# A last part in another order, its mask partly added before the exponential, and one Gelu layer moved by three steps

## The chip, the core and the metric

The kernel runs on one core of a Trainium2 chip. The metric is the time of one execution on the device in microseconds (us); it is the median of several runs. TensorE (PE) multiplies matrices into PSUM, which has eight banks of 512 f32 per partition; VectorE (DVE) and ScalarE (ACT) read PSUM and SBUF; GpSimd (POOL) works on SBUF alone; SyncE (SP) issues most transfers. Each engine executes its own instructions in the order in which they were issued and waits for the others by semaphores.

## What is computed

Everything is f32. There are four batches of 256 query tokens with 256 channels and 4096 context tokens with 192 channels. Each batch goes through three parts, each added to its input:

```python
x = x + cross(norm(x), ctx)   # 16 heads of 16, 4096 keys; scores clipped to +-10000, softmax
x = x + self(norm(x))         # q and k normed by head; causal mask; softmax
x = x + slots(norm(x))        # below
# slots: h = gelu([x, mean slot] @ w1 + b1); logits = h @ w2 (64 slots)
#   alpha = softmax over the 8 best logits, 0 elsewhere
#   slot input = alpha^T x / alpha's column sums; one GRU step on the 64 slots
#   the slots attend to each other, norm, a projection; out = alpha @ slot values @ wo
```

The cross attention also replaces all its weights by 1/4096 if any of them is not a number.

## The kernel before

There are two programs in one. `fast` computes everything with softmaxes that subtract no maximum: it takes the exponential of the scores as they are, multiplies by the values beside a column of ones, and so has numerator and denominator in one sum. `exact` (L215 to L850) computes everything again from the inputs, with the maximum subtracted and the scores clipped. Between them stand these lines:

```python
    redo = fast(tc, a, out, k, const, x0)      # L879
    with tc.If(redo > 0):
        exact(tc, a, out, k)
```

`redo` is a count. Whenever `fast` divides by a softmax's denominators, it also copies them from PSUM into its tile `dens` (128 x 256: batch, which attention, channel half, token half, head). `tile_divide` (L1930) does so for one token half: from the bank it reads 8 denominators per partition and channel half (columns 16, 48, 80 ... 240), writes the quotients to `s.att`, and returns a function that copies the same columns of the same bank to `dens` when it is called. In `ending`, the names `put`, `put0` and `put1` are such functions. `all_in_range` (L1675) compares each entry of `dens` with 1e-10 and 1e15 and makes a 1 for every partition that has an entry outside; `count_bad` (L1687) adds these up by a matmul into `nbad`, which all engines load at the end as `redo`.

`exact` has, for each batch, two passes over the 4096 context tokens in eight chunks of 512. A chunk has 4 key tiles, 2 channel halves and 2 head groups, so 16 blocks of 128 x 1024 scores. In the first pass ACT copies the block to SBUF and DVE makes three tensor_tensor of 128 x 1024 (running maximum, a comparison of the block with itself, the maximum of these). Then POOL takes the maximum over the partitions (two `partition_all_reduce` of 128 x 2048 per batch). In the second pass DVE clips the block (a tensor_scalar from PSUM) and subtracts the maximum (a tensor_tensor), ACT takes the exponential, and PE multiplies by the values. Both passes use two PSUM buffers in turn, for scores, keys and values alike. A sum over all context chunks follows, then self attention token tile by token tile, and the slots part for all batches.

`fast` is one long loop. Per batch it has 16 pairs of key tiles ("pairs", p), and from the second batch on one more step (p = 6) for the self attention of the batch before. In each pair PE makes the scores (L165), ACT the exponentials (L1778, L1780), PE the products with the values of the pair before (L179). Everything else of the batch before (norms, projections, Gelu layer, routing, slots) is spread over these pairs by `plan`, keyed by batch, pair and place in the pair. An even pair also makes the next chunk's keys (L80, L86; moved to SBUF by DVE L94 and ACT L95), an odd one its values (L107, L120). The Gelu layer (`x2_turned`, then `hidden`, L1414) stands at pairs 9 and 10. ACT holds one table of functions; a change between Exp, Gelu and Sqrt is an instruction of its own (ACT_TABLE_LOAD).

In the last batch (b = 3) the last pairs work on token halves: pairs 13 to 16 use `tile_block` (L1876 to L1890) and `tile_weigh` (L1900). Pair 15 ends the first half's cross attention (`tile_out`), pair 16 begins its self attention (`tile_in`). `ending` (L2174) does the rest without any more cross scores to fill PE: the second half's cross attention, the self attention of both halves (`first_*`, `second_*`), norm, Gelu layer, routing (`chosen`), slot inputs, GRU (`gates`), slot attention, and the outputs of all four batches that are still due (`given_out`, `send`). `fill` issues matmuls on zeros. `banks` is one PSUM tile of eight banks; `x_0 ... w_1` are its banks, and the order of PE, DVE and ACT is exactly the order of the code.

Of the kernel before, what the change touches and what calls it, by code (L numbers as in the profile page):

```python
# [19 lines left out]
H, D = 16, 16  # L20
# [880 lines left out]
def fast_(es, tc, nc, a, out, k, const, x0):  # L901
# [180 lines left out]
    tri = kept.tile([P, P], F32, name="tri")  # L1082
    lng = kept.tile([D, 4], F32, name="lng")
# [44 lines left out]
    def set_plain(bank):  # L1128

        for i in range(2):  # L1130
            for c in range(2):
                w = wqkv[:, c, i * C : (i + 1) * C].rearrange("p (h d) -> p h d", d=D)
                m = small.tile([P, H], F32, name="wmean", tag="wmean")
                nc.vector.tensor_reduce(m, w, AX.X, ALU.add)
                nc.vector.tensor_scalar(m, m, 1.0 / D, None, ALU.mult)
                nc.vector.tensor_tensor(
                    w, w, m.unsqueeze(2).to_broadcast([P, H, D]), ALU.subtract
                )

        nc.tensor.transpose(bank[:, 0:P], tri, ident)  # L1140
        nc.vector.tensor_scalar(tri, bank[:, 0:P], 0.0, None, ALU.is_ge)
        for v in vself:
            ones_beside(nc, v)
        nc.vector.memset(sumto, 1.0 / C)
# [339 lines left out]
    def alpha_turned(s, bank):  # L1484
# [7 lines left out]
        nc.scalar.copy(s.two.alphaT[r], bank[r, 0:NQ])  # L1492
# [167 lines left out]
    def given_out(s, bank):  # L1660

        for t in range(QT):
            to = bank[:, t * C : (t + 1) * C]
            nc.tensor.matmul(
                to, ident, s.x2[:, t, :], start=(t == 0), stop=False, skip_group_check=True
            )
        for t in range(QT):
# [50 lines left out]
    for b in range(B - 1):  # L1718
# [20 lines left out]
            ((9, 0), step(x2_turned, s)),  # L1739
            ((HIDDEN_AT, 0), step(hidden, s)),  # L1740
# [152 lines left out]
    def tile_weigh(blocks, c, bank):  # L1893

        for k_, (v_, n, pr) in enumerate(blocks):
# [75 lines left out]
    def tile_stats(src):  # L1971
# [3 lines left out]
        nc.vector.bn_aggr(mv, st)  # L1975
        return mv

    def tile_variance(s, t):
# [4 lines left out]
        mv, var = tile_stats(s.xo[:, t, :]), s.var_t[:, t, 2 * H :]  # L1983
        nc.vector.tensor_scalar(var, mv[:, 1:2], EPS, BIG, ALU.add, ALU.min)
        nc.vector.tensor_scalar(s.eps_t[:, t : t + 1], var, EPS, None, ALU.mult)
# [15 lines left out]
    def tile_v(s, t, bank):  # L2001
        product(
            bank[:, 0:C],
            lambda c: s.x1T[:, c, t * P : (t + 1) * P],
            lambda c: wqkv[:, c, 2 * C : 3 * C],
        )
# [8 lines left out]
    def tile_heads(s, t, sq):  # L2015

        nc.vector.tensor_reduce(
            s.var_t[:, t, 0 : 2 * H], sq.rearrange("p (h d) -> p h d", d=D), AX.X, ALU.add
        )

# [8 lines left out]
    def tile_qk_turned(s, t, q, k_, *engines):  # L2029

        for i, bank in enumerate((q, k_)):
            for c in range(2):
                nc.tensor.transpose(
                    bank[:, c * P : (c + 1) * P],
                    s.qk[:, t, i * C + c * P : i * C + (c + 1) * P],
                    ident,
                )
        at = slice(t * P, (t + 1) * P)
        for dst, bank, i, eng in (
            (s.sq[:, :, 0, at], q, 0, engines[0]),  # L2040
            (s.sq[:, :, 1, at], q, 1, engines[1]),
            (s.sk[:, :, at], k_, 4, engines[2]),
        ):
            src = bank[:, 0 : 2 * P].rearrange("p (c q) -> p c q", c=2)
            j = i + (1 if i == 4 else 2)
            g, b_ = gb[:, i : i + 1], gb[:, j : j + 1]
            if eng is nc.vector:
                nc.vector.tensor_scalar(dst, src, g, b_, ALU.mult, ALU.add)
            else:
                nc.scalar.activation(dst, src, AF.Identity, bias=b_, scale=g)  # L2050
# [9 lines left out]
    def first_scores(s, pairs):  # L2060

        prs = []
        for c in range(2):
            for h in range(2):
                for m in range(2):
                    r = pair_rows(h, m)
                    nc.tensor.matmul(
                        pairs[h][:, m, c * NQ : (c + 1) * NQ],
                        s.sk[r, c, 0:P],
                        s.sq[r, c, :, 0:P],  # L2070
                        start=True,
                        stop=True,
                    )
        for h in range(2):
            pt = pp.tile([P, 2, 2 * NQ], F32, name="prob", tag="prob")
            nc.scalar.activation(pt, pairs[h], AF.Exp)
            prs.append(pt)
        return prs

    def first_weigh(s, prs, bank):  # L2080
        for c in range(2):
            for h in range(8):
                g, m, e = h // 4, h // 2 % 2, h % 2
# [4 lines left out]
                    prs[g][:, m, c * NQ + e * P : c * NQ + (e + 1) * P],  # L2088
# [5 lines left out]
    def second_scores(s, c, h, pair, j):  # L2094

        for m in range(2):
            r = pair_rows(h, m)
            nc.tensor.matmul(
                pair[:, m, j * NQ : (j + 1) * NQ],
                s.sk[r, c, j * P : (j + 1) * P],  # L2100
                s.sq[r, c, :, P:],
                start=True,
                stop=True,
            )

# [8 lines left out]
    def second_weigh(s, prs, c, bank):  # L2114
        for j in range(2):
            for h in range(8):
                g, m, e = h // 4, h // 2 % 2, h % 2
# [4 lines left out]
                    prs[g][:, m, j * NQ + e * P : j * NQ + (e + 1) * P],  # L2122
# [10 lines left out]
    def tile_out(x_0, x_1, y_0, y_1):  # L2133
# [14 lines left out]
        tile_variance(s, 0)  # L2148
# [7 lines left out]
    def tile_in(x_0, x_1, y_0, y_1):  # L2156
# [3 lines left out]
        tokens_turned(x_0, s.xo, 0)  # L2160
        tokens(s.x1T, x_0, 0, nc.vector.tensor_copy)
        alpha_turned(d, y_1)
# [3 lines left out]
        sq = tile_qk(s, 0, x_1)  # L2166
        tile_v(s, 0, y_0)
        tile_heads(s, 0, sq)
        heads_ = s.var_t[:, 0, 0 : 2 * H]
        nc.vector.tensor_scalar(heads_, heads_, 1.0 / D, s.eps_t[:, 0:1], ALU.mult, ALU.add)  # L2170
        s.rs0 = rsqrt(s.var_t[:, 0, :])
        tile_factors(s, 0, x_1, s.rs0[:, 0 : 2 * H])

    def ending(blocks, *pairs):  # L2174
# [24 lines left out]
        tile_weigh(blocks, 1, x_0)  # L2199
        tile_add(s, 1, x_0, 1)  # L2200
        tile_qk_turned(s, 0, z_0, z_1, act, act, act)
        tile_v_moved(s, 0, y_0, s.rs0[:, 2 * H :])


        for c, bank in enumerate((w_0, w_1)):
            tile_turn(tile_of(s.sums[c], 1), bank)
# [3 lines left out]
        for put in puts:  # L2210
            put(vec.tensor_copy)
        prs = first_scores(s, (z, w))
        project(s, wo, x_0, 1)
        tile_residual(s, x_0, 1)
        preload(AF.Sqrt)


        tokens_turned(y_1, s.xo, 1)
        tokens(s.x1T, y_1, 1, vec.tensor_copy)
        tile_mask(prs[0].rearrange("p m (u q) -> p m u q", q=P))  # L2220
        tile_variance(s, 1)
        sq = tile_qk(s, 1, x_1)
        tile_mask(prs[1].rearrange("p m (u q) -> p m u q", q=P))
        tile_v(s, 1, x_0)
        var = s.var_t[:, 1, :]
        rs = small.tile([P, 2 * H + 1], F32, name="rs_t", tag="rs_t", bufs=1)
        act.activation(rs[:, 2 * H :], var[:, 2 * H :], AF.Sqrt)
        tile_heads(s, 1, sq)
        nc.vector.tensor_scalar(
            var[:, 0 : 2 * H], var[:, 0 : 2 * H], BIG, None, ALU.min  # L2230
        )
        act.activation(
            rs[:, 0 : 2 * H], var[:, 0 : 2 * H], AF.Sqrt, bias=s.eps_t[:, 1:2], scale=1.0 / D
        )
        nc.vector.reciprocal(rs, rs)
        tile_factors(s, 1, x_1, rs[:, 0 : 2 * H])
        first_weigh(s, prs, z_0)
        sums0 = as_sums(z_0, 4, act.copy)
        preload(AF.Exp)
        for c in range(2):  # L2240
            tile_turn(sums0[:, 2 * c : 2 * c + 2, :], z_1, c)
        fill(w_0, 0.86)
        tile_qk_turned(s, 1, y_0, y_1, vec, vec, act)
# [3 lines left out]
        put(vec.tensor_copy)  # L2247


        for j in range(2):  # L2250
            for h, pair in enumerate((x_, y)):
                second_scores(s, 0, h, pair, j)
        p0 = [second_exp(pair) for pair in (x_, y)]
        tokens_turned(w_0, s.att, 0)
        with_abo(0)
        tokens(s.attT, w_0, 0, vec.tensor_copy)
        residual(0, w_1)
        second_mask(p0[0])
        p1 = []
        for h, pair in enumerate((x_, y)):  # L2260
            for j in range(2):
                second_scores(s, 1, h, pair, j)
            p1.append(second_exp(pair))
        project(s, awo, w_1, 0, alone=False)
        second_mask(p0[1])
        mv0 = tile_stats(w_1[:, 0:C])
        rs2 = small.tile([P, 2], F32, name="rs2_t", tag="rs2_t", bufs=1)
        nc.vector.tensor_scalar(rs2[:, 0:1], mv0[:, 1:2], EPS, BIG, ALU.add, ALU.min)
        with_abo(1)
        second_weigh(s, p0, 0, z_0)  # L2270
        sums0 = as_sums(z_0, 2, vec.tensor_copy)
        second_mask(p1[0])
        preload(AF.Sqrt)
        residual(1, w_0)
        act.activation(rs2[:, 0:1], rs2[:, 0:1], AF.Sqrt)
        second_mask(p1[1])
        second_weigh(s, p1, 1, z_1)
# [262 lines left out]
```

## Time and profile before

| what | us |
|---|---|
| median of three runs (850.6 to 852.13) | 851.98 |
| the profiled execution | 850.88 |
| its span in the profile | 849.1 |
| PE busy in the span | 826.4 |
| ACT busy | 606.0 |
| DVE busy | 307.3 |

The profile shows `fast` alone: none of its groups comes from the lines of `exact`. It is read from the page's shares first, then from the chain of waits, which follows the work that ended last back from the end, and then from the timeline of the stretches that the change touches. From 0 to about 780 us the chain stays on PE; from there to the last output transfer, issued at 842.93 us, it goes from engine to engine.

### The profile page before, as it was taken

What the parts mean: (1) busy time and instruction counts of PE and PEld (TensorE: products, weight loads), DVE (VectorE), ACT (ScalarE), POOL (GpSimd) and SP (SyncE); (2) the same over time, 40 slices, a digit from 0 to 9 for tenths busy, and PEclk for the clock granted to TensorE, in tenths of its full rate; (3) what the DMA queues carried; (4) which work ended last, traced back from release to release, by engine and by line L of the source; (5) the groups of instructions that cost most, each with busy time, mean ns of one, the idle gap of its engine ahead of it and who ended that gap; (6) DMA issues with size and microseconds to landing.
All of it is one profiled execution on the core that took longest, in us unless ns stands there. A gap on an engine that the chain in (4) does not pass through costs nothing.

```text
span 849.1 us, 19377 instructions
## 1 busy us (share of the span) xinstructions
PE 826.4 (97%) x8403; PEld 451.4 (53%) x8403; DVE 307.3 (36%) x776; ACT 606.0 (71%) x841; POOL 16.8 (2%) x20
## 2 busy tenths in 40 slices
PE   8999999999999999999999999999999999999886
PEld 5445555545555545545545555554545554567564
DVE  3123234222263353212253353232344442113654
ACT  5776776767677768777778777766778777777542
POOL 1000100000000010000000010000000000000000
PEclk9999999999999999999999999999999999999999
DMA  7601001000000000000000000000000000000001
GB/s 205 138 27 50 26 22 55 27 26 25 26 26 26 2 26 26 26 25 27 27 25 26 2 26 26 26 25 10 19 25 26 27 25 25 2 3 2 2 1 54
DMA packets 21822, 25.86 MB, mean 30 GB/s; under 512 B 6241, under 2 KB 13281, under 8 KB 21729
## 3 DMA queue, kind: packets, MB, share of 16 engines
q1 hardware_dynamic: 20784, 23.75, 9.6%
q8 instruction: 68, 1.11, 0.5%
q10 hardware_dynamic: 848, 0.79, 0.3%
q14 instruction: 26, 0.21, 0.1%
q0 software_dynamic: 96, 0.01, 0.0%
HBM read 23.48 MB, written 1.05 MB: 29 GB/s over the span
## 4 chain that ended last, share of the span: by engine, by line
PE 93%; DVE 3%; ACT 2%; issue 1%; DVEq 0%; ACTq 0%
PE banks L165 28%; PE banks L179 25%; PE banks L993 7%; PE banks L80 7%; PE banks L107 7%; PE banks L86 4%; PE banks L120 4%; PE banks L1876 2%; PE banks L1900 1%; PE banks L981 1%; PE banks L1843 1%; PE banks L1058 1%; PE banks L1812 1%; PE banks L194 1%; ACT prob L1780 1%; PE banks L1461 1%
## 5 line engine op out<-in xcount | busy, mean ns | idle before, releaser
L1780 ACT ACTIVATE prob<-banks 128x1024 f32<-128x1024 f32 x360 | 343.8, 1043 | 0.0
L165 PE MATMUL banks<-qh,kt 32*128 32x512 f32 x1920 | 250.2, 620 | 1.2 <-DVE qh L1036 1.2
L179 PE MATMUL banks<-prob,v 128*32 128x256 f32 x3840 | 219.6, 381 | 0.8 <-ACT prob L1822 0.5
L1778 ACT ACTIVATE prob<-banks 128x512 f32<-128x512 f32 x240 | 130.3, 595 | 121.7 <-PE banks L165 121.4
L179 PEld LDWEIGHTS banks<-prob,v 128*32 128x32 f32 x3840 | 118.6, 110 | 117.0 <-ACT prob L1778 42.8
L165 PEld LDWEIGHTS banks<-qh,kt 32*128 32x128 f32 x1920 | 97.6, 183 | 111.1 <-issue 62.5
L1794 DVE TENSOR_TENSOR sums<-banks,sums 128x512 f32<-128x512 f32 x112 | 77.1, 691 | 178.4 <-PE banks L179 155.8
L107 PE MATMUL banks<-wv,ctx 128*128 128x256 f32 x256 | 61.6, 384 | 0.0
L80 PE MATMUL banks<-ctx,wk 128*128 128x512 f32 x128 | 61.5, 603 | 0.1
L107 PEld LDWEIGHTS banks<-wv,ctx 128*128 128x128 f32 x256 | 46.8, 190 | 14.2 <-ACT prob L1778 6.8
L150 DVE COPY v<-banks 128x512 f32<-128x512 f32 x35 | 23.9, 691 | 81.6 <-PE banks L120 77.2
L94 DVE TENSOR_SCALAR kt<-banks,bk 128x512 f32<-128x512 f32 x32 | 24.0, 751 | 66.9 <-PE banks L86 66.8
L150 ACT COPY v<-banks 128x512 f32<-128x512 f32 x29 | 17.0, 587 | 30.0 <-PE banks L120 28.8
L120 PE MATMUL banks<-wv,ctx 64*128 64x256 f32 x256 | 36.3, 402 | 0.0
L86 PE MATMUL banks<-ctx,wk 64*128 64x512 f32 x128 | 36.1, 641 | 0.0
L95 ACT ACTIVATE kt<-banks,bk 128x512 f32<-128x512 f32 x32 | 22.1, 690 | 17.9 <-PE banks L86 17.1
L80 PEld LDWEIGHTS banks<-ctx,wk 128*128 128x128 f32 x128 | 20.9, 189 | 21.2 <-ACT prob L1780 12.1
L120 PEld LDWEIGHTS banks<-wv,ctx 64*128 64x128 f32 x256 | 22.0, 186 | 11.1 <-issue 9.3
L1822 ACT ACTIVATE prob<-banks 128x512 f32<-128x512 f32 (+1 forms) x30 | 17.9, 693 | 8.5 <-PE banks L1812 8.5
L987 DVE COPY tmp<-banks 128x512 f32<-128x512 f32 x17 | 11.8, 691 | 32.8 <-PE banks L981 32.8
L1890 ACT ACTIVATE prob<-banks 128x1024 f32<-128x1024 f32 x24 | 22.9, 1043 | 0.0
L993 PE MATMUL banks<-wqkv,tmp 128*128 128x256 f32 (+1 forms) x56 | 19.6, 482 | 0.5 <-ACT prob L1822 0.5
(310 smaller groups left out, 601.4 us busy)
## 6 DMA issues: line engine op xcount, KB each, us to landing
ctx<-in_ctxT SPq DMA_DIRECT2D x32, 256.0 KB, 3.0
ctx<-in_ctxT SPq DMA_DIRECT2D x64, 128.0 KB, 3.2
x<-in_x SPq DMA_DIRECT2D x4, 256.0 KB, 3.3
wih<-in_ffn_WihT SPq DMA_DIRECT2D x1, 768.0 KB, 7.1
tmp<-in_ffn_WhhT SPq DMA_DIRECT2D x3, 256.0 KB, 4.1
out<-tmp SPq DMA_DIRECT2D x3, 256.0 KB, 2.4
wq<-in_L_xattn_Wq ACTq DMA_DIRECT2D x1, 256.0 KB, 5.6
wo<-in_L_xattn_Wo SPq DMA_DIRECT2D x1, 256.0 KB, 4.7
```

Source lines behind the costliest of these rows:

```text
L80: nc.tensor.matmul(pk[c], k.wk[:, 0, c * P : (c + 1) * P], cx[:, 0, :], start=True, stop=False)
L86: nc.tensor.matmul(pk[c], k.wk[left(c), 1, c * P : (c + 1) * P], cx[left(c), 1, :], start=False, stop=True,)
L94: nc.vector.tensor_scalar(kt[:, 0, :], pk[0], k.bk[:, 0:1], None, ALU.add)
L107: nc.tensor.matmul(pv[n // 2][:, n % 2, :], cx[:, 0, n * P : (n + 1) * P], k.wv[:, 0, :], start=(n % 2 == 0), stop=False, skip_group_check ...
L120: nc.tensor.matmul(pv[u][:, i, :], cx[left(u), 1, n * P : (n + 1) * P], k.wv[left(u), 1, :], start=False, stop=True, skip_group_check=True,)
L150: copy(v[:, :, 0 : H * VW].rearrange("p i (h w) -> p i h w", w=VW)[:, :, :, 0:D], src.rearrange("p i (h d) -> p i h d", d=D),)
L165: nc.tensor.matmul(sc[:, m, :], kt[r, c, i * P : (i + 1) * P], qh[r, c, :], start=True, stop=True)
L179: nc.tensor.matmul(po[q * 32 : (q + 1) * 32, s * NQ : (s + 1) * NQ], v[:, i, w0 : w0 + 32], pr[s][:, m, e * NQ : (e + 1) * NQ], start=(fir ...
L993: nc.tensor.matmul(dst, lhs(c), rhs(c), start=(c == 0), stop=(c == 1))
L1778: nc.scalar.activation(pt[:, m, :], sc[:, m, :], AF.Exp)
L1780: nc.scalar.activation(pt, sc, AF.Exp)
L1794: nc.vector.tensor_tensor(s.sums[c], bank, s.sums[c], ALU.add)
```

## The change

The change has four parts. (1) The third batch's `x2_turned` moves from pair 9 to pair 12 and its `hidden` from pair 10 to pair 13, behind the keys of the last chunk (a new place 3). (2) `tile_in` takes the roots by ACT's table instead of the DVE iteration and uses other banks. (3) `ending` is reordered: scores, exponentials and weighing by head group; for two of the four second-half blocks the causal mask is a summand that PE puts into the bank before the scores (`second_hidden`); the `fill` calls in it are gone; the tables are loaded ahead of their use. (4) The outputs of batches 0 and 1 move forward, and `residual_out` is split off `given_out`. The diff, cut to its core:

```diff
+        nc.vector.tensor_scalar(
+            hidden_by, tri, 2.0**100, -(2.0**100), ALU.mult, ALU.add
+        )
...
-            ((9, 0), step(x2_turned, s)),
-            ((HIDDEN_AT, 0), step(hidden, s)),
+            ((9 if b < B - 2 else 12, 0), step(x2_turned, s)),
+            ((HIDDEN_AT, 0) if b < B - 2 else (13, 3), step(hidden, s)),
...
+    def tile_roots(s, t, sq):
+
+        var = s.var_t[:, t, :]
+        rs = small.tile([P, 2 * H + 1], F32, name="rs_t", tag="rs_t", bufs=1)
+        nc.scalar.activation(rs[:, 2 * H :], var[:, 2 * H :], AF.Sqrt)
         nc.vector.tensor_reduce(
-            s.var_t[:, t, 0 : 2 * H], sq.rearrange("p (h d) -> p h d", d=D), AX.X, ALU.add
-        )
+            var[:, 0 : 2 * H], sq.rearrange("p (h d) -> p h d", d=D), AX.X, ALU.add
+        )
+        nc.vector.tensor_scalar(var[:, 0 : 2 * H], var[:, 0 : 2 * H], BIG, None, ALU.min)
+        nc.scalar.activation(
...
+    def second_hidden(pair):
 
         for m in range(2):
             nc.tensor.matmul(
+                pair[:, m, NQ : 2 * NQ],
+                ident,
+                hidden_by.unsqueeze(1).to_broadcast([P, 2, P]),
                 start=True,
+                stop=False,
+                skip_group_check=True,
+            )
...
         tokens_turned(x_0, s.xo, 0)
+        move = alpha_turned(d, x_1, True)
         tokens(s.x1T, x_0, 0, nc.vector.tensor_copy)
-        alpha_turned(d, y_1)
...
-        sq = tile_qk(s, 0, x_1)
+        sq = tile_qk(s, 0, x_0)
         tile_v(s, 0, y_0)
-        tile_heads(s, 0, sq)
-        heads_ = s.var_t[:, 0, 0 : 2 * H]
-        nc.vector.tensor_scalar(heads_, heads_, 1.0 / D, s.eps_t[:, 0:1], ALU.mult, ALU.add)
-        s.rs0 = rsqrt(s.var_t[:, 0, :])
-        tile_factors(s, 0, x_1, s.rs0[:, 0 : 2 * H])
+        move()
+        s.rs0 = tile_roots(s, 0, sq)
+        preload(AF.Exp)
+        nc.vector.reciprocal(s.rs0, s.rs0)
+        tile_factors(s, 0, x_0, s.rs0[:, 0 : 2 * H])
...
-        fill(w_0, 0.86)
-        tile_qk_turned(s, 1, y_0, y_1, vec, vec, act)
+        for i, bank in enumerate((w_0, w_1)):
+            tile_turned(s, 1, i, bank)
+        tile_moved(s, 1, 0, w_0, vec)
+        tile_moved(s, 1, 1, w_0, vec)
+        tile_moved(s, 1, 4, w_1, act)
...
+        second_hidden(y)
+        second_scores(s, 1, 1, y, True)
+        p11 = second_exp(y)
+        preload(AF.Sqrt)
+        second_mask(p01)
+        second_weigh(s, p00, 0, 0, w_0)
+        second_weigh(s, p01, 0, 1, w_0)
+        second_mask(p10)
+        sums0 = as_sums(w_0, 2, vec.tensor_copy)
+        project(s, awo, x_0, 0, (0,), alone=False)
+        second_weigh(s, p10, 1, 0, w_1)
+        second_weigh(s, p11, 1, 1, w_1)
+        tile_turn(sums0, z_0)
+        sums1 = as_sums(w_1, 2, vec.tensor_copy)
+        residual(1, w_0)
+        put0 = tile_divide(s, z_0, (0,), 1, 1)
+        tile_turn(sums1, z_1)
...
-        tile_turn(sums0, x_0)
-        put0 = tile_divide(s, x_0, (0,), 1, 1)
-        tile_turn(sums1, y_0)
-        tokens_turned(x_1, s.att, 1, (0,))
-        tokens(s.attT, x_1, 1, act.copy, (0,))
-        put1 = tile_divide(s, y_0, (1,), 1, 1)
+        tokens_turned(y_0, s.att, 1, (0,))
+        tokens(s.attT, y_0, 1, act.copy, (0,))
+        put1 = tile_divide(s, z_1, (1,), 1, 1)
         tokens_turned(y_1, s.att, 1, (1,))
...
-        gelu0 = hidden_product(0, x_1)
-        fill(y_1, 0.43)
-        tokens_turned(z_1, s.x2n, 1)
+        gelu0 = hidden_product(0, w_1)
+        tokens_turned(z_0, s.x2n, 1)
+        preload(AF.Gelu)
         gelu0()
-        tokens(s.x2nT, z_1, 1, vec.tensor_copy)
+        tokens(s.x2nT, z_0, 1, vec.tensor_copy)
+        logits(s, 0, x_1[:, 0:SLOTS])
+        gelu1 = hidden_product(1, z_1)
+        gelu1()
+        preload(AF.Exp)
+        act.copy(s.x2[:, 0, :], x_0[:, 0:C])
         act.copy(s.x2[:, 1, :], w_0[:, 0:C])
-        hidden_product(1, w_1)()
-        with_bias(s, "x2", s.x2, fbo)
         put0(vec.tensor_copy)
         put1(vec.tensor_copy)
...
-        slot_inputs(d, z_0, z_1)
-        fill(x_1, 0.86)
+        slot_inputs(d, w_1, z_0)
+        given_out(batches[0], y_0)
         finish(route)
-        slot_inputs(s, y_1, w_0)
-        alpha_turned(s, w_1)
-        finish(gates(both_, x_1, z_1, y_0))
+        with_bias(s, "x2", s.x2, fbo)
+        slot_inputs(s, z_1, x_1)
+        alpha_turned(s, w_0)
+        finish(gates(both_, w_1, z_0, y_1))
         check_range = all_in_range()
         next(check_range)
-        given_out(batches[0], x_0)
-        slot_qk(both_, y_1, w_0)()
+        residual_out(batches[1], x_0)
+        given_out(batches[1], x_0)
...
         finish(mixing)
+        preload(AF.Sqrt)
         move()
-        kept_slots(both_, z_1)
-        at_turned(both_, y_1)
-        given_out(batches[1], z_0)
-        count_bad(y_0)
+        kept_slots(both_, w_1)
+        at_turned(both_, z_1)
+        count_bad(y_1)
...
+            take(3, y[:, 1, :])
             take(4)
```

## The prediction

> **What bounds the kernel now.** The page first: PE is busy for 97% of the span, and all of it is `fast`; no line of `exact` is among the groups.
>
> ```profile
> span 849.1 us, 19377 instructions
> PE 826.4 (97%) x8403; PEld 451.4 (53%) x8403; DVE 307.3 (36%) x776; ACT 606.0 (71%) x841; POOL 16.8 (2%) x20
> ```
>
> Then the chain of waits, in order of time. Up to 780 us it lies on PE, but for places such as the Gelu layer of pair 10, where ACT loads two tables and PE's next products (L179) start at 721.33:
>
> ```profile
> 714.73 2.86 ACT prob L1780 x3
> ...
> 717.60 1.28 ACT L1414
> ...
> 718.90 0.47 ACT hT L1414
> ...
> 719.39 1.28 ACT L1778
> ...
> 720.68 0.60 ACT prob L1778
> ```
>
> Behind 780 it changes engine at almost every step, and PE's own order costs time too: the reader sees two matmul groups of an output (L1664, L1646) between the transpose L1583 and its consumer L1600.
>
> ```profile
> 835.48 0.33 PE banks L1583
> 835.81 0.87 PE banks L1664 x4
> 836.67 1.06 PE banks L1646 x4
> 837.73 0.12 PE banks L1688 x2
> 837.85 0.66 PE banks L1600 x4
> ```
>
> Last the timeline around the two deferred copies of denominators (L1942), because the change gives them other banks:
>
> ```profile
> 818.92 0.42 DVE L1952 COPY tmp<-banks 128x256 f32<-128x256 f32 x1 [0.94 <-PE banks L1946]
> 819.04 0.37 ACT L2328 COPY x<-banks 128x256 f32<-128x256 f32 x1
> 819.26 0.23 DVE L1942 COPY dens<-banks 128x8 f32<-128x8 f32 x2
> ```
>
> They run behind the copy of x2n's transposes. Before, they read x_0 and y_0, which hold the turned sums until the logits go there (L1417, 819.95).
>
> **The change, part by part: the order.** *Gelu layer.* Pair 10's step from L179 to L179 falls from 12.33 (709.00 to 721.33) to the plain odd pair's 10.56 (731.94 to 742.50): -1.77. At pair 13 PE waits in the trace for the keys' copies (751.18 to 752.13); hidden's matmuls (1.06) will fill that. But ACT will do, after its keys (751.89), a load, Gelu and a load (1.28 + 0.47 + 1.28 and gaps: 754.98) before the first exponential, whose half (0.60) is done at 755.6, and L1900 waits for it: from 754.07 to 755.6, +1.5. Exponentials have caught up by the next block, as ACT idles 1.8 there. The transposes (0.59) only change place. Net -0.2; with no catching up +1.
>
> *tile_in.* qk no longer waits behind alpha for the exponential of y (782.79): 783.41 becomes 782.5. Square, reduce, root by table (1.28 load + 0.5) and reciprocal end the factors at 788.5, not 790.04; weighing covers most of it, so 0.5 is kept at the copy of attT (792.40).
>
> *The reordered ending.* Projecting between two halves of the first scores gives 1.0; the sums copied by halves and no fill (0.86) in front of the q and k transposes 0.9; two masks fewer on DVE (0.69 each) against two matmul pairs of 1.06 for the summand, and weighing by head group, 0.7. The second token's x2n ends at about 814.9, not 817.99: -3.1. Logits follow on the same pattern, -3.0.
>
> *Outputs.* `given_out(batches[0])` stands in front of the exponentials of the routing: ACT takes its copy first, so PE's 1.34 + 1.06 and the copy's 0.59 lie before them. The gain shrinks to -1.6 at alpha. Behind the slot attention the two groups of 0.87 and 1.06 shown above go to an earlier wait: -1.6. Sum of the order: -0.2 - 1.6 - 1.6 = -3.4; bounds -6 and +3.
>
> The tables weigh against this: the row shows 1.28 and the next ACTIVATE 0.02 later. The Trainium skill ("ScalarE: Activation LUTs", "What ACT_TABLE_LOAD costs") has a drain of 1.38 beside each; with it the two added loads would cost 2.7 us more, and the order would gain about 1.
>
> **What the order does to the data.** `put0` now reads z_0, `put1` z_1, still at the end of the norm. By then `tokens_turned(z_0, s.x2n, 1)` has overwritten all 256 columns of z_0, and `hidden_product(1, z_1)` the first 128 of z_1. DVE executes the copy of x2n's transposes from z_0 just before put0, as in the timeline above, so put0 can't come earlier. It thus writes into `dens` 8 x 128 values of x2n. A normed token has mean zero over its channels, so about half of these are negative and fail >= 1e-10: `least` is 1 on nearly every partition, `nbad` about 128, `redo` > 0, and `exact` runs behind all of `fast`. No number above hides that; it is added whole.
>
> **What `exact` costs.** No row shows it; I count its instructions and price them by the nearest rows. There are 4 x 8 x 4 x 2 x 2 = 512 blocks in each pass.
>
> ```profile
> L2053 DVE TENSOR_TENSOR prob<-prob,tri 128x1024 f32<-128x1024 f32 x2 | 2.4, 1216 | 0.0
> ...
> L150 DVE COPY v<-banks 128x512 f32<-128x512 f32 x35 | 23.9, 691 | 81.6 <-PE banks L120 77.2 <-ACT prob L1890 4.5
> ```
>
> - DVE passes: 3 + 2 = 5 operations of 128 x 1024 per block, 2560. A tensor_tensor takes 1.216, and the next can begin 1.13 after it (796.63 to 797.76). The clip from PSUM: 0.691 for 512 columns and (1.216 - 0.688) for 512 more, 1.22, the same. ACT needs 1.04 per block, PE 0.25 per score matmul (L165) and 0.06 per record of L179, some 1 us per block: both hidden. 2560 x 1.13 = 2893 if all overlap, x 1.25 = 3200 if each waits for the one before. I take 1.16, near the overlapped row, since the two kinds alternate: 2970.
> - DVE per chunk: 64 halves of keys x 0.75 + 32 of values x 0.69 = 70.
> - Chunk borders of the second pass: keys and values take PE 3.0 each (748.15 to 751.18, 759.71 to 762.70) in the two buffers that the scores need; DVE has some 4 of other work meanwhile. 0 to 6 each; I take 2 x 32 = 64.
> - POOL's maximum over partitions: 8 of 128 x 2048, with DVE waiting. POOL's 128x512 takes 1.27, so one pass over 2048 is 5.1; seven halvings of 128 partitions would be 36. Geometric middle 14: 112 (41 to 288). Clip and memset of 128x4096 around it: 20.
> - The rest, with rows of the same shapes: inputs, norm and queries 27; context sums 32 x 2.4 (two buffers, 3.0 landing, 1.2 reduce) = 77; projection, norm, q and k 88; self attention 32 groups x 4.5 (DVE 1.9 to 3.3, ACT 2.3 to 3.0, half hidden) = 143; output projection 12; slots part 92. 439, bounds 300 and 600.
>
> Sum: 2970 + 70 + 64 + 112 + 20 + 439 = 3675. All low ends give 3324, all high 4370.
>
> **The total** is made against the profiled execution, 850.88 (0.13% under the median 851.98): 850.88 - 3.4 + 3675 = 4522; rounded up for the branch, 4530. The medians' 1.1 is nothing beside that.
>
> **Rivals.**
> 1. *`exact` doesn't run* (not slower). It needs `dens` to hold only values in range: if the copies saw the turned sums still in z_0 and z_1. For it speaks only that the bank's names are easily misread; against it the order of DVE's instructions. Then the order alone decides: 850.88 - 3.4 = 847.5, or 848.6 at the median, faster by 0.4%. It decides as soon as no value written is out of range.
> 2. *`exact` runs but isn't bound by DVE.* If PE fell to half clock in the passes, its 2.65 per pair of blocks (4 x 0.25 + 16 x 0.056 + 6.0 / 8) would be 5.3 against DVE's 4.6, +0.7 x 256 = 180 in the second pass; with POOL at its upper bound +176. 4530 + 356 = about 4890. For it: POOL's price is unknown, and PE is busy for a sixth of the first pass. Against: a busier PE should recover, and the granted clock stays at 1.00 in this trace until 845.1, 3.2 after the last matmul; PE's gaps in the first pass are 3.4 - 0.5 = 2.9. The Trainium skill ("TensorE: Matmul & The Clock Gate", "What's actually happening") halves the clock after an idle window of about 3.4; by that rule the clock would hold, just, and this rival would lose its first half.
> 3. *`exact` runs at the fast ends*: 1.13 per operation (-77), no border stalls (-64), POOL 41 (-71), the rest 380 (-59): 4530 - 271, about 4260.
> 4. *No `exact`, and the order loses*: pair 13 doesn't catch up and half-empty gaps of 2.4 without fill slow PE: up to 854.
>
> **How the numbers follow.** Chances: the forecast, 4330 to 4900, 0.80; above it (rival 2 and worse) 0.09; below, still with `exact` (rival 3), 0.06; rival 1 0.04; rival 4 0.01. The range 4330 to 4900 is the forecast's own: from three quarters of the way to rival 3 up to rival 2. Slower by over 0.2% (1.7 us, about what a measurement can tell from no change): 0.80 + 0.09 + 0.06 + 0.005 = 0.955; faster 0.04; within 0.2% 0.005. The predicted time is 4530.
>
> **What would show it.** In the profile after: lines L377 to L406 head the groups, tensor_tensor of 128x1024 by the 1500, DVE busy over 80%, PE below 60% of the span; POOL with eight long operations, which give its price. The step between two first-pass blocks is 3.4 to 3.5 and between two pairs of the second 4.6. The `fast` part ends its last DVE addition near 839, not 842.9; the Gelu layer's load stands behind the keys of pair 13. Wrong it would be by a span near 846 with no line of `exact`, or by a POOL operation far outside 5 to 36.

## The result, and the profile after

The changed kernel takes 4624.2 us (median of four runs, 4615.21 to 4626.31) against 851.64 before (850.6 to 852.13): 5.4286 times as long, 95% interval 5.4192 to 5.438. The profiled execution took 4615.21, with a span of 4613.4. The page (shares and the row of the granted clock in 40 slices):

```profile
span 4613.4 us, 47479 instructions
...
PE 3433.4 (74%) x18909; PEld 1337.1 (29%) x18909; DVE 3584.8 (78%) x3998; ACT 1836.9 (40%) x2309; POOL 161.2 (3%) x94
...
PEclk9999999655558775555787555577865556886697
```

There are 2.5 times as many instructions as before, and from the eighth slice (of 115 us) on the clock is another: this is where `fast` ends. The costliest groups of DVE and POOL (columns: line, tiles, count, then busy time, mean ns, and idle time before):

```profile
L378 DVE TENSOR_TENSOR top<-top,raw 128x1024 f32<-128x1024 f32 x512 | 623.6, 1218 | 71.3 <-ACT raw L377 71.3
...
L402 DVE TENSOR_SCALAR gprob<-ring 128x1024 f32<-128x1024 f32 x512 | 603.9, 1215 | 13.7 <-PE ring L165 13.4
...
L383 POOL PARTITION_ALL_REDUCE shift<-top x8 | 83.9, 10539 | 2907.6 <-DVE top L378 2907.6
```

L215 to L850 are `exact`, of which the page before had no line. The timeline of the changed kernel's DVE shows what calls it:

```profile
816.65 0.42 DVE L1965 COPY tmp<-banks 128x256 f32<-128x256 f32 x1 [0.53 <-PE banks L1959]
817.00 0.16 DVE L1955 COPY dens<-banks 128x8 f32<-128x8 f32 x1
818.80 0.17 DVE L1955 COPY dens<-banks 128x8 f32<-128x8 f32 x1 [1.65 <-ACT hT L2372]
```

The first line reads x2n's transposes from z_0; the next, `put0`, takes its 8 "denominators" from the same bank. The third, `put1`, even waits 1.65 for the hidden product that ACT reads in z_1. Time by stage (columns: stretch, its length, busy time and instructions of PE, weight loads, DVE, ACT, POOL, then granted clock, DMA share, GB/s). The four rows are the first and the second pass of the first batch, the context sums, and all the rest of `exact`:

```profile
879.20:1356.00 476.80, 289.88 (x594) 79.61 (x592) 448.25 (x395) 135.12 (x137) 21.04 (x2) 0.53 0.03 9
1356.00:1715.20 359.20, 298.77 (x1720) 92.03 (x1720) 307.00 (x284) 145.90 (x145) 0.00 (x0) 0.79 0.04 12
...
4206.00:4290.00 84.00, 11.28 (x28) 4.71 (x20) 43.42 (x57) 0.00 (x0) 0.00 (x0) 0.50 0.55 175
4290.00:4613.40 323.40, 240.19 (x1214) 188.37 (x1214) 197.19 (x431) 105.72 (x335) 55.41 (x64) 0.78 0.08 23
```

`fast` ends its last addition at 844.60 (843.91 and 0.69); 34.6 go into `exact`'s loads, norm and queries; the eight passes take 3326.8 (four of about 477, four of about 356); then 84.0 and 323.4. So nearly all of the difference is `exact` (3768.8 to the span's end). But the last addition of `fast` is also later than the 842.90 of before, where the prediction had it near 839. The experiments go after both.

### The profile page after: what moved, and what is told of

The parts are those of the page before. It is cut to its first block, busy times and chain, and to the rows that moved or that the text cites. A ratio compares the mean times of both kernels' runs of the same rounds, so it can differ in the third digit from the quotient of the medians.

```text
span 4613.4 us, 47479 instructions
## 1 busy us (share of the span) xinstructions
PE 3433.4 (74%) x18909; PEld 1337.1 (29%) x18909; DVE 3584.8 (78%) x3998; ACT 1836.9 (40%) x2309; POOL 161.2 (3%) x94
## 4 chain that ended last, share of the span: by engine, by line
DVE 50%; PE 36%; ACT 6%; issue 3%; POOL 3%; DMA 1%; SPq 0%; ACTq 0%; DVEq 0%; POOLq 0%
DVE top L378 12%; DVE ne L379 12%; DVE nan L380 12%; PE ring L165 7%; DVE gprob L402 6%; PE banks L165 5%; ACT gprob L406 5%; PE banks L179 5%; DVE gprob L403 4%; PE po L179 3%; POOL shift L383 2%; PE ring L80 2%; PE ring L86 1%; PE banks L993 1%; PE banks L80 1%
## 5 line engine op out<-in xcount | busy, mean ns | idle before, releaser
L165 PE MATMUL ring<-qh,kt 32*128 32x512 f32 x4096 | 1533.0, 998 | 729.6 <-ACT raw L377 506.5
L377 ACT COPY raw<-ring 128x1024 f32<-128x1024 f32 x512 | 515.1, 1012 | 1093.9 <-DVE ne L379 1046.6
L165 PEld LDWEIGHTS ring<-qh,kt 32*128 32x128 f32 x4096 | 424.6, 269 | 1644.4 <-ACT raw L377 1168.3
L406 ACT ACTIVATE gprob<-gprob 128x1024 f32<-128x1024 f32 x512 | 541.0, 1057 | 678.6 <-DVE gprob L403 508.1
L378 DVE TENSOR_TENSOR top<-top,raw 128x1024 f32<-128x1024 f32 x512 | 623.6, 1218 | 71.3 <-ACT raw L377 71.3
L379 DVE TENSOR_TENSOR ne<-raw 128x1024 f32<-128x1024 f32 x512 | 623.5, 1218 | 0.0
L380 DVE TENSOR_TENSOR nan<-nan,ne 128x1024 f32<-128x1024 f32 x512 | 623.3, 1217 | 0.0
L402 DVE TENSOR_SCALAR gprob<-ring 128x1024 f32<-128x1024 f32 x512 | 603.9, 1215 | 13.7 <-PE ring L165 13.4
L403 DVE TENSOR_TENSOR gprob<-gprob,shift 128x1024 f32<-128x1024 f32 x512 | 604.7, 1217 | 2.0
L179 PE MATMUL po<-gprob,g_v 128*32 128x256 f32 x4096 | 403.3, 473 | 220.2 <-ACT gprob L406 215.2
L179 PEld LDWEIGHTS po<-gprob,g_v 128*32 128x32 f32 x4096 | 88.8, 120 | 689.7 <-ACT gprob L406 646.8
L179 PE MATMUL banks<-prob,v 128*32 128x256 f32 x3840 | 219.6, 381 | 0.5 <-ACT prob L1834 0.5
L179 PEld LDWEIGHTS banks<-prob,v 128*32 128x32 f32 x3840 | 118.6, 110 | 116.7 <-ACT prob L1790 42.5
```

The costliest lines, as they stand in the source:

```text
L165: nc.tensor.matmul(sc[:, m, :], kt[r, c, i * P : (i + 1) * P], qh[r, c, :], start=True, stop=True)
L179: nc.tensor.matmul(po[q * 32 : (q + 1) * 32, s * NQ : (s + 1) * NQ], v[:, i, w0 : w0 + 32], pr[s][:, m, e * NQ : (e + 1) * NQ], start=(fir ...
L377: nc.scalar.copy(raw, sc)
L378: nc.vector.tensor_tensor(half, half, raw, ALU.max)
L379: nc.vector.tensor_tensor(ne, raw, raw, ALU.not_equal)
L380: nc.vector.tensor_tensor(nan, nan, ne, ALU.max)
```

## The experiments

**The banks alone.** `own_banks` is the changed kernel with these lines:

```diff
-        tokens_turned(z_0, s.x2n, 1)
+        tokens_turned(y_1, s.x2n, 1)
-        tokens(s.x2nT, z_0, 1, vec.tensor_copy)
+        tokens(s.x2nT, y_1, 1, vec.tensor_copy)
-        gelu1 = hidden_product(1, z_1)
+        gelu1 = hidden_product(1, w_1)
```

> The two deferred copies of denominators get their banks for themselves: x2n's second transposes go to y_1 and the second hidden product to w_1, so z_0 and z_1 still hold the turned sums when they are copied. Theory A (the overwritten banks are what calls the fallback): no line of exact in the profile, a span near 850 instead of 4613. Rival (something else in the new order calls it, for instance the mask as a summand of 2^100, which could leave a denominator out of range): still near 4620. Under A this run also shows the order alone: by the prediction's terms 3.4 faster than before, ratio 0.996; by the trace of the changed kernel, whose last addition of the fast part ends 1.7 later than before (0.67 of it from the first microseconds), 1.0 to 1.7 slower, ratio 1.001 to 1.002.

Measured: 852.26, ratio 1.001 (1.0 to 1.002), and no line of `exact`. The rival with the mask falls. The order alone, then, gains nothing: of its two expectations the trace's (1.0 to 1.7 slower) came near, with 0.7 slower, and the prediction's -3.4 failed.

`before_overwritten` does the opposite in the kernel before:

```diff
-        tokens_turned(z_1, s.x2n, 1)
+        tokens_turned(x_0, s.x2n, 1)
-        tokens(s.x2nT, z_1, 1, vec.tensor_copy)
+        tokens(s.x2nT, x_0, 1, vec.tensor_copy)
-        hidden_product(1, w_1)()
+        hidden_product(1, y_0)()
```

> The kernel before, in its old order, with one thing of the change: x2n's second transposes go to x_0 and the second hidden product to y_0, the two banks that its deferred copies of denominators read afterwards. Theory A (the overwritten banks alone cost the time): exact runs in full, 851.6 plus the 3772 that lie between the changed kernel and own_banks, about 4624. Rival (the fallback's length belongs to the new order too): anything more than 20 away from that, or 852 if the old order copies in time.

Measured: 4618.3 in one run (before, on that chip, 850.84). `one_bank` has the first two lines of `own_banks` only:

> The changed kernel with only put0's bank kept: x2n's second transposes go to y_1, the second hidden product stays in z_1, of which it overwrites the first 128 of 256 columns before put1 copies its 8. Theory A: four of the eight copied columns hold products ahead of the Gelu, about half of them negative, so exact runs: 4624. Rival (only the x2n values in z_0 are out of range): about 852.

Measured: 4621.93 in one run. The product in z_1 alone is enough (z_0 alone wasn't tried), and the old order with overwritten banks costs the same. The cause is settled.

**Why the order gained nothing.** In the changed kernel's trace the clock reads 0.5 from 822.56 to 829.39, and PE's 24 gate matmuls take 3.70 instead of 2.94. In `own_banks` it is worse. Its stretches of 3.41, the steps in which the clock's records change (columns as above):

```profile
816.31:819.72 3.41, 2.15 (x17) 1.72 (x16) 1.04 (x7) 2.36 (x5) 0.00 (x0) 1.00 0.00 0
819.72:823.14 3.42, 3.42 (x14) 3.03 (x13) 1.85 (x11) 1.33 (x4) 1.26 (x1) 0.50 0.00 0
823.14:826.55 3.41, 1.08 (x4) 0.44 (x3) 1.04 (x4) 1.07 (x3) 0.00 (x0) 0.50 0.22 77
826.55:829.96 3.41, 3.41 (x17) 2.96 (x16) 1.07 (x3) 0.00 (x0) 0.00 (x0) 0.50 0.00 0
829.96:833.38 3.42, 3.42 (x17) 3.42 (x17) 0.85 (x2) 0.78 (x2) 0.00 (x0) 0.50 0.00 0
```

In the first of them PE was busy for 2.15 of 3.41, with no gap longer than 0.81, and the next four stretches ran at half clock, one of them with the wait of 2.33 for alpha in it. The change had taken the three `fill` calls out of this part. Three kernels ask which gap matters, each with one edit on `own_banks`:

```diff
# routing_first
-        given_out(batches[0], y_0)
         finish(route)
+        given_out(batches[0], y_0)
# fill_gap
         given_out(batches[0], y_0)
+        fill(w_0, 1.72)
# fill_both: fill_gap and
         gelu1 = hidden_product(1, w_1)
+        fill(y_1, 0.43)
```

> own_banks with the routing's exponentials and divisions ahead of the output of the first batch on ACT; PE's order is unchanged. In the changed kernel's trace the exponentials start at 822.17 behind the copy of that output, and could start at 820.80: alpha and the slot inputs 1.37 earlier. If the wait of 2.33 in front of the slot inputs is what halves the clock at 822.56, it shrinks to about 1.0, the clock holds, and a further 2.5 to 3.5 come back: 3.9 to 4.9 faster than own_banks. If the clock is lost for another reason: 1.4 faster than own_banks at most, and the matmuls of L1466 still take 1.9 per eight.

> own_banks with eight idle matmuls (2.1 us at full clock) behind the output of the first batch, where PE waits 2.33 for alpha. Theory (this wait halves the clock): the granted clock stays at 1.00 through the slots part, 24 gate matmuls take 2.9 instead of 3.7, 2.5 to 3.5 faster than own_banks. Rival (the clock is decided by the gaps before 821, 0.81 and 0.46 long around the hidden products): the clock still falls at about 822.6, and the time is that of own_banks or up to 0.3 slower.

> fill_gap with two more idle matmuls between the second hidden product and the second logits, where the kernel before has them. If the wait for alpha alone decides the clock: as fill_gap, up to 0.2 slower for the later logits. If the gaps before 821 decide it: 2.5 to 3.5 faster than own_banks where fill_gap is not.

| kernel | us | ratio to before | granted clock from 815 to 840, profiled execution |
|---|---|---|---|
| `own_banks` | 852.26 | 1.001 (1.0 to 1.002) | 0.5 for 13.65 |
| `routing_first` | 850.77 | 0.9987 (0.9978 to 0.9996) | 0.5 for 10.24, then 3.41 |
| `fill_gap` | 848.02 | 0.9957 (0.9943 to 0.9971) | 0.5 for 3.41, ahead of alpha |
| `fill_both` | 847.73 | 0.9956 (0.9942 to 0.9969) | 1.0 throughout |

`routing_first` is 1.5 faster than `own_banks`, which the earlier exponentials alone would give (1.37): in its trace the wait for alpha is gone, and still the clock falls, at 818.93, with PE continuously busy behind it. So there it isn't the wait for alpha that drops the clock, and the gaps around the hidden products are what is left. In the profiled execution of `fill_gap` the clock falls as well (0.5 from 820.95), but the eight idle matmuls lie inside the fall, and the clock is back before alpha. That execution is the slowest of five (849.24). Three of the others have a mean granted clock of 0.999, which has no room for a fall of 3.41 (it alone makes 0.998), so there filling the wait for alpha was enough. `fill_gap` is 4.2 faster than `own_banks`; my rival for it was right on the clock of one execution and wrong on the time. Which of the gaps decides in a given execution is not shown. With `fill_both`, which also fills one of the gaps around the hidden products, the clock of the profiled execution never falls (same columns):

```profile
816.73:820.15 3.42, 3.40 (x25) 2.87 (x24) 1.95 (x11) 2.37 (x5) 0.28 (x1) 1.00 0.00 0
820.15:823.56 3.41, 3.00 (x16) 2.12 (x15) 1.33 (x5) 1.07 (x3) 0.98 (x1) 1.00 0.22 77
```

Its median is 0.3 under that of `fill_gap`, which the intervals can't tell apart, so the expected difference between the two did not come. That the lost clock is what the order paid with shows in the mean granted clock of all executions: 0.989 to 0.993 in the eleven of `own_banks` (850.61 to 853.91), 0.997 to 0.999 in the five of `fill_both` (847.65 to 848.47), in the same order but for ten matmuls on zeros. The kernel before loses the clock at times too: of its 21 executions beside these, twenty have 0.996 to 0.998, and the slowest, 854.26, has 0.992.

**The Gelu move, and a better order.** In another set of runs on one chip `fill_both` ran once more beside three kernels built on it. `gelu_back` returns `x2_turned` and `hidden` of the third batch to pairs 9 and 10. `both_orders` adds `routing_first`'s swap, with `fill(w_0, 0.86)` instead of 1.72. `copies_early` adds to that:

```diff
         gelu0()
+        act.copy(s.x2[:, 0, :], x_0[:, 0:C])
+        act.copy(s.x2[:, 1, :], w_0[:, 0:C])
...
-        act.copy(s.x2[:, 0, :], x_0[:, 0:C])
-        act.copy(s.x2[:, 1, :], w_0[:, 0:C])
...
-        fill(w_0, 0.86)
+        fill(w_0, 0.43)
```

> fill_both once more, as the base of the three kernels beside it on the same chip. Theory: 3.6 to 4.0 faster than before, as in its first run (ratio 0.9956). If that gain was the chip's and not the kernel's: a ratio outside 0.994 to 0.997.

> fill_both with the third batch's Gelu layer back at pair 10, as in the kernel before; the ending stays reordered. The prediction gives the move a net of -0.2: 1.77 saved at pair 10, 1.5 lost at pair 13. Theory A: 0 to 0.4 slower than fill_both. Rival (the move is worth its whole 1.77, since the exponentials catch up): 1.5 to 1.8 slower. Second rival (it costs, up to the prediction's +1): 0.5 to 1.0 faster than fill_both.

> fill_both with the routing's exponentials ahead of the first batch's output on ACT, and four idle matmuls instead of eight behind it, as the wait for alpha is then about 1.0. In fill_both's trace the exponentials start at 821.17 and could start at 819.80. Theory: the clock holds, alpha comes 1.37 earlier, all behind it with it: 1.2 to 1.4 faster than fill_both, ratio to before about 0.994. Rival (another wait takes its place, or the shorter filling lets the clock fall): within 0.3 of fill_both or slower.

> both_orders with ACT's two copies of x2 (0.35 each) between the two Gelus, where ACT idles 1.03, instead of ahead of the routing's exponentials, and two idle matmuls instead of four. Theory: the exponentials start right behind the table load, 0.5 earlier, and alpha with them: 0.3 to 0.5 faster than both_orders. Rival (the second Gelu or DVE's top values come last): within 0.2 of both_orders.

| kernel | us | ratio to before (851.5) |
|---|---|---|
| `fill_both_again` | 848.17 | 0.9952 (0.9934 to 0.997) |
| `gelu_back` | 848.46 | 0.9961 (0.9946 to 0.9975) |
| `both_orders` | 847.75 | 0.9947 (0.9928 to 0.9966) |
| `copies_early` | 846.96 | 0.994 (0.9918 to 0.9962) |

The Gelu move is worth 0.3 by the medians, which the intervals can't tell from nothing. Executions differ by up to 1.4 in when the warm-up ends, so traces are compared from the first product of L179: from there to the last addition `fill_both_again` needs 814.29 (840.63 - 26.34), `gelu_back` 814.32 (839.76 - 25.44). `fill_both_again` kept its ratio inside the expected 0.994 to 0.997. `both_orders` missed its 1.2: it is 0.4 faster by the medians. In its profiled execution alpha does come earlier, but the clock falls at 833.13 for 3.41, so part of the gain went back. That execution is the slowest of seven, though (849.3, mean clock 0.996); the other six have 0.998, and why they miss the 1.2 stays open. `copies_early` is the fastest kernel of this study, 4.5 under before; it is 0.8 under `both_orders`, more than the 0.3 to 0.5 expected, but the intervals of the two overlap.

**What bounds `exact`.** The first pass in the changed kernel's timeline:

```profile
1001.00 1.22 DVE L380 TENSOR_TENSOR nan<-nan,ne 128x1024 f32<-128x1024 f32 x1
...
1001.12 2.08 PE L165 MATMUL ring<-qh,kt 32*128 32x512 f32 x4 [1.33 <-ACT raw L377]
1002.14 1.22 DVE L379 TENSOR_TENSOR ne<-raw 128x1024 f32<-128x1024 f32 x1
1003.27 1.22 DVE L378 TENSOR_TENSOR top<-top,raw 128x1024 f32<-128x1024 f32 x1
```

DVE begins an operation every 1.13 to 1.14 and waits for nothing. PE's four matmuls take 2.08 (1.13 in a block of the second pass at a clock of 1.00, shown further below), as the clock is at a half, 0.53 over the whole pass; PE then waits 1.33 for a buffer. `no_nan_max` leaves L380 out:

> The changed kernel with one DVE operation per block of the fallback's first pass left out, the maximum that collects the flags of NaN (L380; NaN inputs are then not found), 512 in all. Theory A (DVE bounds the first pass, and PE's half clock there costs nothing): the step from block to block falls from 3.41 to 2.27, the whole by 512 x 1.136 = 582, to about 4042. Rival (PE at half clock is next in line: 2.08 of matmuls per block and the copy of 1.01 behind them): the step stays at 2.6 or more, the whole falls by less than 415.

Measured: 4060.95, 563 less. The first pass fell from 476.8 to 335.6 (879.6 to 1215.2, with the first clip of the second pass in it), by 141.2 where 128 x 1.136 is 145.4, and the step is 2.27 (1001.42 to 1003.68 in its timeline) with PE still at 2.08. DVE bounds the pass, and the half clock costs nothing there. A busier PE did not bring the clock back either: in these 335.6 PE was busy for 284.64, and the clock read 0.56. `three_rings` gives `exact` a third score buffer:

```diff
-            name="g4", bufs=4
-        ) as g4, tc.tile_pool(name="g_ring", bufs=2, space=PSUM) as ring, ...
+        ) as g4, tc.tile_pool(name="g_ring", bufs=3, space=PSUM) as ring, ...
...
-                pv = pm.tile([P, C], F32, name="pm", tag="pm")
+                pv = two_banks()[:, 0, 0:C]
```

> The changed kernel with three score buffers in the fallback instead of two (the one product of the context means uses one of them, which frees the bank). In the changed kernel DVE idles 249 at chunk borders: 71 in front of L378, 85 in front of L94, 79 in front of L150, 14 in front of L402. Theory A, the prediction's (keys and values take the two buffers that the scores need): most of it goes, 4624 falls by 120 to 220. Rival (at a border PE's own work is what lasts: keys 5.7 at half clock behind the last scores): the time stays within 40.

Measured: 4772.15, 148 slower, which neither theory had. The wait at borders did not shrink (L94 111 instead of 85, L150 95 instead of 81), L402 now waits 128 for PE instead of 14, and the first three second passes took 401, 386 and 401 instead of 359, 356 and 356. Its timeline inside a chunk:

```profile
1417.65 2.35 DVE L402 TENSOR_SCALAR gprob<-ring 128x1024 f32<-128x1024 f32 x2 [1.74 <-PE ring L165]
1418.50 2.07 PE L165 MATMUL ring<-qh,kt 32*128 32x512 f32 x2
...
1420.50 1.08 PE L179 MATMUL po<-gprob,g_v 128*32 128x256 f32 x8
...
1423.68 1.23 DVE L402 TENSOR_SCALAR gprob<-ring 128x1024 f32<-128x1024 f32 x1 [1.41 <-PE ring L165]
```

Two blocks take 6.03 here, not 4.53: with three buffers the scores and the value products stand in another order on PE, and at half clock PE, not DVE, sets the step. This run also changed PE's order, so it tells the buffers from the border's own work less cleanly than meant; what can be said is that more buffers in this order did not help.

## Why the prediction was right, and where its sum was off

*What the order does to the data* held as far as the runs show it: the copies come behind the overwriting, and `exact` runs behind all of `fast`; how many entries fail the comparison was not measured. The likeliest case was the one that happened, and 4624 lies in its range.

*What `exact` costs*, term by term, predicted against measured:

| term | predicted | measured | from |
|---|---|---|---|
| 2560 DVE operations | 2970 | 2907 | 1.1355 each, the step of the first pass divided by 3 |
| keys and values on DVE | 70 | 61 | L94 32 x 2 and L150 32, by their steps of 0.66 and 0.6 |
| chunk borders | 64 | 251 | idle time before L94 85, L150 81, L378 71, L402 14 |
| POOL's maximum | 112 | 48 | eight operations of 10.5, 84 in all; DVE's wait before L389 |
| clip and memset | 20 | 21 | 4 x 2.21 + 3 x 3.39, and 0.8 ahead of each memset; the first memset lies in the 34.6 |
| batch ends | not counted | 39 | what is left of the 3326.8 |
| the rest | 439 | 442 | 34.6 + 84.0 + 323.4 |
| sum | 3675 | 3769 | |

The step that was mis-sized is *chunk borders of the second pass*: 2 for each was taken from bounds of 0 to 6, and the trace shows 180 in the second passes (L94, L150, L402), some 5.8 for each of 31, the upper end. It also left out that the first pass has borders: 71, or 2.23 each. The chain of the changed kernel at a border shows the order in which it happens:

```profile
1435.21 2.01 PE ring L165 x4
1437.22 3.50 PE ring L80 x4
1440.72 0.57 PE po L179 x8
1441.29 1.05 PE ring L86 x2
```

The keys' first matmuls take 3.50 here, with the clock at a half until 1440.37, where `fast` has 1.92: the 3.0 was read at full clock. But the clock is not all of it. These are DVE's waits for the keys of this border, and for keys and values at the next one, where the clock is at 1.00:

```profile
1444.00 0.75 DVE L94 TENSOR_SCALAR kt<-ring,bk 128x512 f32<-128x512 f32 x1 [4.17 <-PE ring L86]
...
1486.69 0.75 DVE L94 TENSOR_SCALAR kt<-ring,bk 128x512 f32<-128x512 f32 x1 [1.19 <-PE ring L86]
1490.46 0.69 DVE L150 COPY g_v<-ring 128x512 f32<-128x512 f32 x1 [3.01 <-PE ring L120]
```

With 0.44 for the next scores the second border costs 4.64, and ten borders of the second passes cost just that; sixteen, with part of them at half clock, cost 6.3 to 7.9. So the 2 was too low at full clock already, and the half clock adds up to 3.2. POOL's geometric middle of 14 was 10.5, and DVE had other operations in its queue for part of the 21 per batch. The errors of +187, -64 and -63 partly cancel; the total was 2% low.

*DVE over 80%, PE below 60%*: DVE is busy for 78% of the span (3281 of 3769 in `exact`, 87%), PE for 74%. Both missed, the first narrowly. PE's share has two reasons. One is that of rival 2: matmuls at half clock are busy twice as long. The other is the price of the scores, "0.25 per score matmul". A matmul of the code has two records (4096 for 1024 blocks of two), and the price came from rows such as the first one here, of `fast` in the trace of before; the second is a block of `exact`, at a clock of 1.00:

```profile
735.53 2.06 PE L165 MATMUL banks<-qh,kt 32*128 32x512 f32 x16
...
1447.65 1.13 PE L165 MATMUL ring<-qh,kt 32*128 32x512 f32 x4
```

Two records take 0.26 in the first and 0.57 in the second, and 1.04 in the first pass at half clock. By the single records, four matmuls start together in `fast` (735.528 to 735.548), and two in this pass (1001.120 and 1001.127); what the difference comes from was not tested. So a block of the first pass costs PE 2.08 and not 0.5, its gap is 1.33 and not 2.9, and PE is busy for 61% of that pass and not for a sixth. A busy share says little where the clock isn't read with it.

*Rival 2, first half.* "A busier PE should recover" was wrong for the first pass (0.53) and half wrong for the second (0.79). Its price, though, did not come: the step stayed at 4.53 for two blocks, also at half clock (1410.16 to 1414.69). `three_rings` shows that it could have, with 6.03 where rival 2 had 5.3. In the kernel before the clock falls 3.0 behind the end of the last matmul (842.06), not 3.2 as the prediction has it. The Trainium skill ("TensorE: Matmul & The Clock Gate", "What's actually happening") has half clock after an idle window of about 3.4. In the trace the clock stays at a half with PE's gaps at 1.33 in the step of the first pass, and in `own_banks` it fell behind a stretch with no gap over 0.81. The measurement decides: no gap of 3.4 is needed.

*The order of `fast`, -3.4.* The Gelu term held (-0.2 predicted, -0.03 between the traces of `fill_both_again` and `gelu_back`). From the first product of L179, the second token's x2n ended 2.54 earlier than before (predicted 3.1). What failed is the sum behind it: counted in the same way, the last addition came 1.03 later, not 3.4 earlier, since the removal of the fillings was costed with the matmuls that it saves and not with the clock that they hold. Rival 4 had that mechanism, at 0.01. With two fillings back the term is there: `fill_both` is 3.9 under before, and its last addition comes 2.56 earlier from the first product of L179 (839.24 - 24.96 against 842.21 - 25.37).

*The tables.* Each added load shows 1.28, as in the trace of before, and the next ACTIVATE follows at once (815.63 and 1.28 make 816.91; it begins at 816.92).

## What to carry to other kernels

Where a helper returns a deferred read of a buffer, list who writes that buffer between the helper and the call before a buffer is renamed: nothing but the values changes, and a kernel with a fallback turns that into time. Matmuls on zeros were no waste here: ten of them took `own_banks` from 852.26 to 847.73. A reordering that removes such matmuls has to be costed with the granted clock of what follows, and not only with the time that they take. And where a fallback or another rare path exists, know its price: here 3772 us hung on two bank names.

## What was not expected of the hardware

The granted clock changed only in steps of 3.41 from its first full-speed record, and that record began at 4.4 in one execution of `fill_both` and at 7.4 in another of the same kernel, so where a step lies against the work is chance. The Trainium skill ("TensorE: Matmul & The Clock Gate", "What's actually happening") gives a free-running window of 3413 ns, which agrees. The spread of `own_banks` goes with the clock: its two fastest executions (850.61 and 850.81) have a mean clock of 0.993, its four slowest (853.79 to 853.91) 0.989. PE busy for 0.63 of such a stretch was followed by half clock in `own_banks`, and 0.73 in the changed kernel (819.14 to 822.56); but the kernel before held 1.00 behind a stretch of 0.56 (814.38 to 817.79, 1.91 of 3.41), and `no_nan_max` stayed near a half with PE busy for 0.85 of a pass. So PE's busy share alone is not what the clock counts; what it does count is left open. A partition_all_reduce of 128x2048 took 10.5 on average.
